# Key bias, mask stores, zeros' products and the router norm's small rows moved in a one-core perceiver kernel

## The chip, the cores and the metric

One Trainium2 chip, one NeuronCore of it. The metric is the device time of one execution in microseconds (us). The kernel of before ran three times: 1151.5 is the median, 1147.58 the lowest, 1159.3 the highest. A profile of one further execution gives every instruction's start and duration. The engines are PE (TensorE; its weight loads are listed as PEld), DVE (VectorE), ACT (ScalarE), POOL (GpSimd) and SP (SyncE, which here issues DMAs).

## The reference, cut to what matters

All in F32. 64 sequences of 32 tokens of 256 features attend to a context of 257 rows of 64 features; two layers of cross attention, self-attention and feed-forward, each ahead of a residual sum and behind a layer norm:

```python
x = x + _L0_xattn_ref(_layernorm(x), ctx_512, ...)
x = x + _L0_attn_ref(_layernorm(x), ...)
x = x + _L0_ffn_ref(_layernorm(x), ...)
x = x + _L1_xattn_ref(_layernorm(x), ctx_512, ...)
x = x + _L1_attn_ref(_layernorm(x), ...)
x = x + _L1_ffn_ref(_layernorm(x), ...)
```

Three of them matter here. `_L0_ffn_ref` picks 4 of 16 blocks of hidden units for each token and masks the others:

```python
prob = jax.nn.softmax(xf @ Wr.T + br, axis=-1)
_, idx = jax.lax.top_k(prob, TOP_K)
mask = mask.at[jnp.arange(n)[:, None], idx].set(1.0)
h = jax.nn.gelu(h, approximate=False) * mask[:, :, None]
```

`_L1_attn_ref` adds a bias to its queries, keys and values (`kg = einsum(x, Wk) + bk`). `_L1_ffn_ref` sends each token to one of 8 experts:

```python
route = jax.nn.sigmoid(x @ router_w)
max_ind = jnp.argmax(route, axis=1)
...
    h = jax.nn.silu(x @ gate_w[e]) * (x @ up_w[e])
    out = out + jnp.where(mask, h @ down_w[e], 0.0)
out = out * max_prob
```

## The kernel before, in words

The 2048 tokens are 16 tiles of 128 (NT = 16), taken in 4 groups of 4 tiles. The stages follow each other on one core, with the times of the profiled execution: first cross attention (to about 129 us), first self-attention with the feed-forward of group 0 woven in (to about 483), the feed-forward of groups 1 to 3 (to about 560), second cross attention in 32 pairs of batches (to about 905), second self-attention with the router (to about 1030), the experts (overlapping it from about 1018), and the last output DMAs.

The order of instructions on PE, DVE and ACT is the order of the source in these stages (`manual_schedule`). POOL's order is also that of the source in the two attentions of the first layer; in the second cross attention and the router POOL's order is not written by hand, and a scheduler chooses it. SP's DMAs wait in one queue.

What the change touches:

*Zeros' products.* `fill(n, bank)` (L562) issues n products of a 128x256 tile of zeros into a PSUM bank that nobody reads. It is called at the start of the first cross attention and in its first steps. Its main loop (L603) runs over t = 0 to 17. A step issues the scores of tile t + 1, a part of the next group's queries and keys, the output projection of tile t − 2 (`ya`, L552), the softmax's row sums, the transposes of tile t − 1's probabilities (`ptp_a`, L280, copied by ACT to `pT_a`, L282), the values of tile t + 1, and the product of probabilities and values of tile t − 1 (`oa`, L523, copied by ACT to `oTa`, L531). In the last steps tiles run out, so less work stands between these. Keys of the next stage are transposed there too (`kTp`, L392).

*Mask stores.* `choose_store(g)` (L705) transposes group g's mask of chosen blocks on PE (`mTp`, L710), copies it on DVE (`mTc`, L712) and stores it to DRAM (`maskd`, L713); `spread` loads it back as 8 broadcast tiles `mb`. A table filled by `at(slot, place, fn)` puts such steps into the slots t = 0 to 16 of the first self-attention's loop (L1136): group 0's store is in slot 9, group 1's in slot 13, both at place 2, which is between the ACT exponential and the output projection `yb` (L979) of tile t − 1. `oTb` (L971, DVE; L973, ACT) is that projection's input. Group 2's store is inside the last tile's projection, after head 11 of 16. The mask itself is finished by `choose_best` (L703 is its last addition).

*Key bias.* `e_bk` (L1725) multiplies the key bias, loaded as small DMAs into `e_b`, with a two-column mask, once, on POOL. The source puts it at pair 20 of the second cross attention. The keys' feature step of the next stage reads it (ACT, `kde`, L1452). In that same cross attention POOL negates each batch's row maximum (`nm`, L1516), which ACT's exponential (`pp`, L1519) uses as a bias; PE then transposes the probabilities (`pt`, L1547), and makes the next pair's queries (`qd`, L1306) and values' products (`np`, L1282).

*Router norm.* The router's layer norm works by groups of four (tiles 0 to 3) or two tiles. `route_stats(t)` makes statistics on DVE; with the last tile of a group it calls `route_scale` (L1793): POOL adds epsilon (L158), takes the power −1/2 (L159), copies the scale into `lnq_f` (L1799), makes minus mean times scale (L1800, L1801) and copies both per tile into the two extra columns of `xf`'s row (L1803), which is sent later to the sorted rows in DRAM. `route_norm` (called a step or more later, at a place of its own in the source) then makes `xn_f` on ACT (L1812) from `lnq_f`; `route_turn` transposes it on PE (`tpf`, L1828) and copies it on ACT (`xTf`, L1833); `route` makes the logits (`lpf`, L1842) and the one-hot choice on DVE (L1851 to L1862); `places` makes each token's rank in its expert on PE (`rank`, L1876), and `send` scatters the row by a POOL DMA (L1896). `give_table` makes on DVE the table of which expert each tile of sorted rows belongs to; its loads follow. `rows_turn` transposes the sorted rows (`tps`, L2214).

Of the kernel before, what the change touches and what calls it, by code (L numbers as in the profile page):

```python
# [7 lines left out]
F32 = mybir.dt.float32  # L8
# [31 lines left out]
def bc(ap, axis, n):  # L40

    shape = list(ap.shape)
    shape.insert(axis, n)
    return ap.unsqueeze(axis).to_broadcast(shape)
# [3 lines left out]
def perceiver_kernel(ctx: ExitStack, tc: tile.TileContext, a: dict, out: bass.AP):  # L48
# [22 lines left out]
    def sm(name, shape):  # L71
        return small.tile(shape, F32, tag=name.split("_")[0], name=name)
# [327 lines left out]
    with tc.tile_pool(name="wA", bufs=2) as work, tc.tile_pool(  # L400
# [75 lines left out]
        def power(t):  # L476
            nc.scalar.activation(sc[t], sc[t], AF.Exp)
# [84 lines left out]
        def fill(n_, bank=warm):  # L562
            for _ in range(n_):
                nc.tensor.matmul(bank, zero[:, 0:P], zero, start=True, stop=True)
# [38 lines left out]
        for t in range(NT + 2):  # L603


            if t + 1 < NT:
                score(t + 1)
            if t == 0:
                for part in (2, 3):
                    norm(1, part, "a", mvs, lat)  # L610
            if t == 2:
                fill(3, ps1.tile([P, 256], F32, tag="PT", name="warm2"))
            group(t // 4 + 1, (2, 0, 1, 3)[t % 4])
            for step in first.get(t, ()):
                step()
            if t > 1:
                project(t - 2)
            if t < NT:
                share(t)
            if t < 2:  # L620
                fill(2 - t)
            if 1 <= t <= NT:
                turned[t - 1] = heads_on_partitions(sc.pop(t - 1), ps1, t - 1, work, "a")
            if t + 1 < NT:
                values(t + 1)
                power(t + 1)
            if 1 <= t <= NT:
                gather(t - 1)
            if t == 14:
                keys_scale(0)  # L630
            if t == 15:
                turn_keys(0, ps2)
            norm(t // 4 + 2, t % 4, "a", mvs, lat)
            if 4 <= t < 11:
                norm_b(t - 4)
            if t == 10:
                rotate_last(work)
# [218 lines left out]
    with tc.tile_pool(name="wB", bufs=2) as work, tc.tile_pool(  # L856
# [118 lines left out]
        def project(t):  # L975
            oT = ctxo.pop(t)
            y_ps = outs[t] = ps_y.tile([P, D], F32, tag="y", name=f"yb{t}")
            for h in range(NH):
                nc.tensor.matmul(  # L979
                    y_ps, oT[:, h, :], b_o[:, h, :], start=(h == 0), stop=(h == NH - 1)  # L980
                )
                if (t, h) == (NT - 1, 11):
                    choose_store(NG - 2, ps2, work)

        def norm_stats(t):
# [68 lines left out]
        def at(slot, place, fn):  # L1054
            steps.setdefault((slot, place), []).append(fn)
# [10 lines left out]
        for g in range(NG - 1):  # L1066
            at(4 * g + 5, 5, lambda g=g: choose_norm(g))
            at(4 * g + 6, 1, lambda g=g: choose_turn(g, ps2, work))
            at(4 * g + 7, 5, lambda g=g: choose_blocks(g, ps2, work))
            if g == NG - 2:  # L1070
                at(4 * g + 8, 5, lambda g=g: choose_best(g, work, (2, 3)))
                continue
            for slot, place_, rounds in ((7, 5, (0,)), (8, 5, (1, 2)), (8, 4, (3,))):
                at(
                    4 * g + slot,
                    place_,
                    lambda g=g, rounds=rounds: choose_best(g, work, rounds),
                )
            at(4 * g + 9, 2, lambda g=g: choose_store(g, ps2, work))
        ff, late = {}, []  # L1080

        def ff_late():
# [312 lines left out]
    with wd1:  # L1395
        wd.close()
        with tc.tile_pool(name="wD", bufs=2) as work, tc.tile_pool(
# [290 lines left out]
            for pair in range(NB // 2):  # L1688


                b = 2 * pair
                if pair % 2 == 0 and pair // 2 + 2 < NT:
                    rotated(pair // 2 + 2)
                if pair == 0:
                    query_part(-1)
                    chain_n(1, ps1)()
                if pair == 3:
                    wdn.close()
                    mbw.close()
                    wc.close()  # L1700
                    wep = ctx.enter_context(tc.tile_pool(name="wep", bufs=1, side="right"))
                    fgp = ctx.enter_context(tc.tile_pool(name="fgp", bufs=1, side="right"))
                    fw.append(fgp.tile([P, NE * FE], F32, name="fg"))
                    we0 = ctx.enter_context(ExitStack())
                    e_w = we0.enter_context(tc.tile_pool(name="wE0", bufs=2, side="right"))
                    vd = [
                        e_w.tile([P, 4, 4, 4, NH + 1], F32, name=f"vde{z}", bufs=1)
                        for z in range(3)
                    ]
                if 2 < pair < 31:  # L1710
                    project((pair - 3) // 2, 4 * ((pair - 3) % 2), 4)
                if pair == 31:
                    project(NT - 2)
                for fn in behind.get(pair - 1, ()):
                    fn()
                turn(b)
                query_part(pair)
                for fn in front.get(pair, ()):
                    fn()
                turn(b + 1)  # L1720
                between(pair + 1)
                if 11 < pair < 28:
                    load_piece()
                if b == 40:
                    nc.gpsimd.tensor_tensor(e_bk, bc(e_b[:, 1], 2, 2), bc(mask2, 1, KC), ALU.mult)  # L1725
                if b == 16:

                    e_q = wep.tile([P, KC, D], F32, name="e_q")
                    by_pairs(e_q, a["e_wq"])
                    e_k = wep.tile([P, KC, D], F32, name="e_k")  # L1730
                    for k in range(KC):
                        for z in range(4):
                            o, w = divmod(z, 2)
                            nc.sync.dma_start(
                                e_k[:, k, o * P : (o + 1) * P].rearrange(
                                    "p (r w d) -> p w r d", r=4, w=2
                                )[:, w],
                                a["e_wk"][k * P : (k + 1) * P, :].rearrange(
                                    "p (r d) -> p r d", r=4
                                ),  # L1740
                            )

                    e_b = wep.tile([P, 2, KC], F32, name="e_b")
                    for z, v0 in enumerate((V_BQ, V_BK)):
                        for o in range(KC):
                            for r in range(4):
                                p0 = 64 * (r % 2) + 32 * o
                                nc.sync.dma_start(
                                    e_b[32 * r : 32 * r + 32, z, o : o + 1],
                                    a["vecs"][p0 : p0 + 32, v0 + r // 2 : v0 + r // 2 + 1],  # L1750
                                )
                    e_bk = wep.tile([P, KC, 2], F32, name="e_bk")
                    e_v = wep.tile([P, KC, DC], F32, name="e_v")
                    nc.sync.dma_start(e_v, a["e_wv"].rearrange("(k p) o -> p k o", p=P))
                    f_r = wep.tile([P, KC, 8], F32, name="f_r")
                    nc.sync.dma_start(f_r, a["f_wr"].rearrange("(k p) o -> p k o", p=P))
# [36 lines left out]
    def route_scale(ts):  # L1793

        n_ = len(ts)
        mv = rows[ts][:, 0:n_, :]
        sc2 = rows[ts] = sm(f"lnq_f{ts[0]}", [P, 4, 2])
        rs = rstd_of(mv, n_, f"f{ts[0]}", True)
        nc.gpsimd.tensor_copy(sc2[:, :n_, 0], rs)  # L1799
        nc.gpsimd.tensor_tensor(rs, rs, mv[:, :, 0], ALU.mult)  # L1800
        nc.gpsimd.tensor_scalar(sc2[:, :n_, 1], rs, -1.0, None, ALU.mult)  # L1801
        for i, t in enumerate(ts):
            nc.gpsimd.tensor_copy(xf[t][:, D + 2 : DP], sc2[:, i, :])  # L1803

    def route_norm(ts, pool=None):
        sc2, rows[ts] = rows[ts], []
        for i, t in enumerate(ts):
            if pool is None:
                y = xnp.tile([P, D], F32, tag="xn", name=f"xn_f{t}")
            else:  # L1810
                y = pool.tile([P, DP], F32, tag="r", name=f"xn_f{t}", bufs=7)[:, :D]
            nc.scalar.activation(  # L1812
                y, xs[t], AF.Identity, scale=sc2[:, i, 0:1], bias=sc2[:, i, 1:2]
            )
            rows[ts].append(y)
# [802 lines left out]
```

## Time and profile before

| | us |
|---|---|
| median of three runs | 1151.5 |
| lowest, highest | 1147.58, 1159.3 |
| the profiled execution | 1156.52 |
| its span, first to last instruction | 1154.6 |
| PE busy | 1106.7 |
| DVE busy | 767.8 |
| ACT busy | 572.7 |
| POOL busy | 463.9 |

The mean granted TensorE clock of the profiled execution is 0.986 of full speed. In the page, a row of the timeline is start, duration, engine, line, operation, output<-inputs, shape, number of instructions, and in brackets the idle time of the engine before it and what ended it. A row of the windows is the stretch, its length, the busy time of PE, PEld, DVE, ACT and POOL with instruction counts, the granted clock, the DMA share and GB/s. A row of the waits is engine and line that waited, what it waited for, the total, how often, and the longest. Matmuls of several instructions are shown as one row with their number behind an x.

The row maximum's negation L1516 on POOL and the exponential on ACT are among the costliest groups (128 and 256 instructions). 7 of L1799, L1800 and L1801 and 16 of L1803 run, between 949.6 and 1033.0.

### The profile page before, as it was taken

The numbers are of one execution on the slowest core, as the hardware profiler recorded it, in microseconds if no ns is written. First come the engines' busy times: TensorE is split into PE (matmuls) and PEld (weight loads), VectorE is DVE, ScalarE is ACT, GpSimd is POOL, SyncE is SP. The second block draws the span as 40 slices with busy tenths as digits, with TensorE's granted clock in tenths as the row PEclk, the third lists the DMA queues.
The fourth block names the chain that finished last, engine by engine and source line by source line (L and its number), as shares of the span: only waits on it lengthen the run. The fifth ranks groups of instructions, "written<-read, shape, count | busy, mean of one in ns | idle before, by whom it ended". The sixth has DMA issues, their size and how long they took to land. (4 is left out here: it accounts for less than half of the span.)

```text
span 1154.6 us, 26411 instructions
## 1 busy us (share of the span) xinstructions
PE 1106.7 (96%) x10036; PEld 792.2 (69%) x10036; DVE 767.8 (67%) x1805; ACT 572.7 (50%) x1433; POOL 463.9 (40%) x778
## 2 busy tenths in 40 slices
PE   9999999999999999999998999999999989889997
PEld 5667867777767657677776777777776656555653
DVE  5787156776987997655236787777878565765532
ACT  2346363545355365232236777777777556542221
POOL 1444266878768687410011121121222355642111
PEclk9999899999999999999999999999999988999999
DMA  5131142545436436591232121223220044212413
GB/s 134 58 95 40 33 124 82 176 126 168 120 109 200 129 106 191 159 257 36 74 83 22 29 55 29 74 56 83 64 76 19 17 125 122 85 36 73 154 39 117
DMA packets 98990, 109.05 MB, mean 94 GB/s; under 512 B 37240, under 2 KB 73465, under 8 KB 98642
## 3 DMA queue, kind: packets, MB, share of 16 engines
q1 hardware_dynamic: 97138, 103.05, 31.5%
q0 software_dynamic: 1728, 4.33, 1.1%
q8 instruction: 80, 1.31, 0.5%
q14 instruction: 44, 0.36, 0.1%
HBM read 76.36 MB, written 31.41 MB: 93 GB/s over the span
## 5 line engine op out<-in xcount | busy, mean ns | idle before, releaser
L1519 ACT ACTIVATE pp<-Sd,nm 128x256 f32<-128x256 f32 x256 | 119.9, 482 | 42.4 <-POOL nm L1516 42.4
L888 PEld LDWEIGHTS qb<-xT_b,b_q 128*128 128x128 f32 x512 | 94.7, 190 | 39.0 <-issue 18.5
L888 PE MATMUL qb<-xT_b,b_q 128*128 128x256 f32 x512 | 121.3, 385 | 0.0
L1516 POOL TENSOR_SCALAR nm<-nm 128x2 f32<-128x2 f32 x128 | 27.0, 211 | 219.4 <-DVE nm L1515 219.2
L979 PE MATMUL yb<-b_o,oTb 128*128 128x256 f32 x512 | 113.6, 380 | 0.5 <-DVE oTb L971 0.5
L1515 DVE TENSOR_REDUCE nm<-Sd 128x2 f32<-128x512 f32 x128 | 79.5, 683 | 50.1 <-PE Sd L1502 50.1
L979 PEld LDWEIGHTS yb<-b_o,oTb 128*128 128x128 f32 x512 | 96.2, 190 | 14.4 <-issue 1.4
L1537 DVE TENSOR_TENSOR pp<-pp,rd 128x512 f32<-128x512 f32 x128 | 89.6, 700 | 4.4
L1553 ACT COPY pTd<-pt 128x512 f32<-128x512 f32 x128 | 68.8, 591 | 10.0 <-PE pt L1547 4.2
L896 ACT COPY qTb<-qb 128x512 f32<-128x512 f32 x64 | 37.5, 585 | 69.8 <-PE qb L888 67.0
L1547 PE MATMUL pt<-cst,pp 128*128 128x128 f32 x512 | 67.8, 273 | 4.4 <-DVE pp L1537 1.7
L907 POOL TENSOR_TENSOR q2b<-qTb 128x512 f32<-128x512 f32 x64 | 64.7, 1042 | 14.6 <-ACT qTb L896 14.6
L1547 PEld LDWEIGHTS pt<-cst,pp 128*128 128x128 f32 x512 | 59.1, 141 | 13.8 <-ACT ld L1527 4.0
L941 DVE RECIPROCAL rqb<-rqb 128x512 f32<-128x512 f32 x16 | 53.5, 3344 | 17.8 <-ACT rqb L936 17.8
L1306 PE MATMUL qd<-xT_d,d_m 128*128 128x256 f32 x256 | 64.3, 395 | 0.7 <-DVE rd L1536 0.3
L1594 PE MATMUL yd<-d_n,co 128*128 128x256 f32 x256 | 63.2, 391 | 0.0
L1528 POOL TENSOR_TENSOR sd<-sd,ld 128x2 f32<-128x2 f32 x128 | 26.9, 210 | 86.0 <-ACT ld L1527 86.0
L1502 PE MATMUL Sd<-ct,qTd 64*128 64x256 f32 x480 | 60.0, 388 | 0.0
L1568 PE MATMUL od<-pTd,na 128*64 128x256 f32 x480 | 58.4, 385 | 0.0
L742 PE MATMUL yc<-c,hc 128*128 128x256 f32 x256 | 58.4, 381 | 0.0
L1594 PEld LDWEIGHTS yd<-d_n,co 128*128 128x128 f32 x256 | 46.2, 189 | 16.7 <-DVE nm L1515 7.7
L955 DVE RECIPROCAL rdb<-denb 128x512 f32<-128x512 f32 x16 | 53.7, 3355 | 5.8 <-PE denb L953 5.6
(433 smaller groups left out, 2426.9 us busy)
## 6 DMA issues: line engine op xcount, KB each, us to landing
srt<-pad SPq DMA_DIRECT2D x17, 1040.0 KB
mb<-maskd SPq DMA_DIRECT2D x64, 128.0 KB
ct<-ctd SPq DMA_DIRECT2D x30, 257.0 KB
rct<-in_ctxT_dram SPq DMA_DIRECT2D x32, 128.5 KB
rrt<-in_ctxT_dram SPq DMA_DIRECT2D x64, 64.2 KB
ctd<-rct SPq DMA_DIRECT2D x32, 128.5 KB
nad<-rna SPq DMA_DIRECT2D x16, 256.0 KB
fg<-in_f_wg_dram SPq DMA_DIRECT2D x16, 256.0 KB
```

The lines of the kernel that those rows point to most:

```text
L742: nc.tensor.matmul(y_ps, hs[f][:, i * P : (i + 1) * P], c_2[:, f, :], start=(f == 0), stop=(f == 7),)
L888: nc.tensor.matmul(q_ps[:, hh, :], b_q[:, k, h * P : (h + 1) * P], xT[:, k, c0 : c0 + 256], start=(k == 0), stop=(k == KC - 1),)
L907: nc.gpsimd.tensor_tensor(q2[:, 4 * h4 : 4 * h4 + 4, :], q, q, ALU.mult)
L979: nc.tensor.matmul(y_ps, oT[:, h, :], b_o[:, h, :], start=(h == 0), stop=(h == NH - 1))
L1306: nc.tensor.matmul(q_ps[:, r, :], m[:, k, pr * P : (pr + 1) * P], xT[:, k, c0 : c0 + 256], start=(k == 0), stop=(k == KC - 1),)
L1502: nc.tensor.matmul(logits[b][hh][:, u, :], qT[hs, b % 8, 4 * u : 4 * u + 4, :], ct[hs, b % 4, :KEYS], start=True, stop=True,)
L1515: nc.vector.tensor_reduce(nm, s_ps[hh], AX.X, ALU.max, negate=True)
L1519: nc.scalar.activation(pb[:, u, hh, :], s_ps[hh][:, u, :], AF.Exp, bias=nm[:, u : u + 1], accum_out=sd[:, u : u + 1],)
L1537: nc.vector.tensor_tensor(pp, pp, bc(rd, 2, KEYS), ALU.mult)
L1547: nc.tensor.transpose(pts[c][:, hh * 256 + u * P : hh * 256 + u * P + P], probs[b][:, u, hh, c * P : (c + 1) * P], ident,)
L1553: nc.scalar.copy(pT[:, c, :], pt)
L1594: nc.tensor.matmul(y_ps, co[:, pr, :], n[:, pr, :], start=(pr == pr0), stop=(pr == pr0 + n_pr - 1),)
```

## The change: what it does

Four parts. First, at step 14 of the first cross attention's loop a spare PSUM tile is allocated, and pairs of zeros' products go ahead of `project(13)` and, at steps 14 and 15, ahead of the product of probabilities and values: six products of 128x256. Second, the mask stores of groups 0 and 1 go one slot later, and that of group 2 after head 15 in place of head 11. Third, the key bias's product goes from POOL to DVE. Fourth, `route_scale` keeps only the addition and the power on POOL; the copy of the scale, the shift (now one instruction in place of two) and the row copies go to DVE, and stand at the head of `route_norm`.

The diff:

```diff
@@ first cross attention, loop over t
+            if t == 14:
+                spare = ps1.tile([P, 256], F32, tag="S", name="warm3")
+            if t == 15:
+                fill(2, spare)
             if t > 1:
                 project(t - 2)
...
+            if t in (14, 15):
+                fill(2, spare)
             if 1 <= t <= NT:
                 gather(t - 1)
@@ first self-attention, project(t)
-                if (t, h) == (NT - 1, 11):
+                if (t, h) == (NT - 1, NH - 1):
                     choose_store(NG - 2, ps2, work)
...
-            at(4 * g + 9, 2, lambda g=g: choose_store(g, ps2, work))
+            at(4 * g + 10, 2, lambda g=g: choose_store(g, ps2, work))
@@ second cross attention
                 if b == 40:
-                    nc.gpsimd.tensor_tensor(e_bk, bc(e_b[:, 1], 2, 2), bc(mask2, 1, KC), ALU.mult)
+                    nc.vector.tensor_tensor(e_bk, bc(e_b[:, 1], 2, 2), bc(mask2, 1, KC), ALU.mult)
@@ route_scale and route_norm
-        sc2 = rows[ts] = sm(f"lnq_f{ts[0]}", [P, 4, 2])
-        rs = rstd_of(mv, n_, f"f{ts[0]}", True)
-        nc.gpsimd.tensor_copy(sc2[:, :n_, 0], rs)
-        nc.gpsimd.tensor_tensor(rs, rs, mv[:, :, 0], ALU.mult)
-        nc.gpsimd.tensor_scalar(sc2[:, :n_, 1], rs, -1.0, None, ALU.mult)
+        rows[ts] = mv, rstd_of(mv, n_, f"f{ts[0]}", True)
+
+    def route_norm(ts, pool=None):
+        n_ = len(ts)
+        mv, rs = rows[ts]
+        sc2, rows[ts] = sm(f"lnq_f{ts[0]}", [P, 4, 2]), []
+        nc.vector.tensor_copy(sc2[:, :n_, 0], rs)
+        nc.vector.scalar_tensor_tensor(
+            sc2[:, :n_, 1], mv[:, :, 0], -1.0, rs, ALU.mult, ALU.mult
+        )
         for i, t in enumerate(ts):
-            nc.gpsimd.tensor_copy(xf[t][:, D + 2 : DP], sc2[:, i, :])
-
-    def route_norm(ts, pool=None):
-        sc2, rows[ts] = rows[ts], []
+            nc.vector.tensor_copy(xf[t][:, D + 2 : DP], sc2[:, i, :])
         for i, t in enumerate(ts):
```

Behind the new lines, line numbers in the changed program are higher: by 4 and 6 from the first cross attention's loop on, by 8 from the router's norm on.

## The prediction

> **What bounds the kernel now.** I read the page's first two parts, then the view of waits for PE, then the windows in which PE is not full, and the timeline at each wait that the change touches.
>
> ```profile
> PE 1106.7 (96%) x10036; PEld 792.2 (69%) x10036; DVE 767.8 (67%) x1805; ACT 572.7 (50%) x1433; POOL 463.9 (40%) x778
> ...
> PEclk9999899999999999999999999999999988999999
> ```
> ```profile
> PE mTp L710 <- DVE maskc L703: 3.9, 2, 2.1
> PE tpf L1828 <- ACT xn_f L1812: 2.5, 2, 2.3
> PE pt L1547 <- ACT ld L1527: 1.6, 1, 1.6
> PE oa L523 <- ACT pT_a L282: 1.3, 2, 0.7
> PE ya L552 <- ACT oTa L531: 1.1, 1, 1.1
> ```
>
> PE is busy 1106.7 of a span of 1154.6, so 47.9 us of idle is all that shorter waits can give. The second row says that busy is not all work: in some slices the granted clock is below full, and the same matmul lasts longer. The waits (total, times, longest) are short and scattered; those shown are the ones at the edited lines, 10.4 us together. So each edit is worth its own wait plus what the clock loses near it. One execution took 1156.52 around that span, 5.0 above the median of 1151.5; the sum below is made on 1156.5 and then moved to the median.
>
> **Zeros' products at the end of the first cross attention.**
>
> ```profile
> 117.99 1.70 PE L552 MATMUL ya<-a_o,oTa 128*128 128x256 f32 x4 [1.08 <-ACT oTa L531]
> 119.48 1.06 PE L280 MATMUL ptp_a<-cst,s_a 128*128 128x128 f32 x4
> 121.22 1.92 PE L523 MATMUL oa<-pT_a,vda 128*64 128x32 f32 x32 [0.68 <-ACT pT_a L282]
> 123.07 1.12 PE L392 MATMUL kTp<-cst,kvb 128*128 128x128 f32 x4
> 123.98 1.65 PE L552 MATMUL ya<-a_o,oTa 128*128 128x256 f32 x4
> 125.47 0.60 PE L280 MATMUL ptp_a<-cst,s_a 128*128 128x128 f32 x4
> ```
> ```profile
> 120.00:130.00 10.00, 9.32 (x93) 7.87 (x92) 2.16 (x6) 1.92 (x4) 1.05 (x1) 0.74 0.00 0
> ```
>
> The times ahead of PE are start and duration. The window's row gives, after the five busy times, the granted clock: 0.74. The ptp group takes 1.06 at 119.48 and 0.60 at 125.47; at full clock ya takes 1.03, oa 1.12 and kTp 0.60. Three pairs of zeros go into the waits for pT_a and oTa. A 128x256 product takes 0.38, a pair 0.76; the waits filled are 0.65, 1.08 and 0.68, so a pair alone overshoots by 0.1 at two of them. If the pairs keep the clock full, 117.99 to 125.47 (7.48) becomes 1.03 + 0.60 + 0.76 + 1.12 + 0.60 + 1.03 = 5.14, a gain of 2.3. What follows is PE-bound query work, so it is carried. Bounds: the whole clock loss of the two windows from 110, (1 − 0.92)·10 + (1 − 0.74)·10 = 3.4; the other way, no effect on the clock and only the overshoot, +0.2. I take −2.3, because the same row shows the clock lost with gaps of no more than 1.08 us and the zeros remove just these.
>
> [...]
>
> **Key bias on VectorE.**
>
> ```profile
> 623.40 0.20 POOL L1725 TENSOR_TENSOR e_bk<-e_b,mask 128x4 f32<-128x4 f32 x1 [2.49 <-DMA f_r<-in_f_wr_dram]
> 623.57 0.21 POOL L1516 TENSOR_SCALAR nm<-nm 128x2 f32<-128x2 f32 x1
> 623.81 0.47 ACT L1519 ACTIVATE pp<-Sd,nm 128x256 f32<-128x256 f32 x1 [1.75 <-POOL nm L1516]
> 625.00 0.63 PE L1547 MATMUL pt<-cst,pp 128*128 128x128 f32 x4 [1.58 <-ACT ld L1527]
> 627.13 3.58 PE L1306 MATMUL qd<-xT_d,d_m 128*128 128x256 f32 x8 [0.16 <-DVE rd L1536]
> ```
>
> Nobody fixes POOL's order in this stage; the bias product (0.20) stood early in its queue and waited 2.49 for a load, with the row-maximum negation nm behind it. ACT waits 1.75 for nm, PE 1.58 for ACT and 0.71 for the next pair, then qd runs at a reduced clock, 3.58 against 1.97 elsewhere. From np to Sd the pair before takes 6.48 (612.20 to 618.68), this one 9.56 (622.39 to 631.95): 3.1 us to win. On DVE the product stands where the source has it, at pair 20, long after its loads have landed, and costs some 0.2 (POOL's row) on an engine that is 67% busy; nothing on PE waits for it there. I take −3.1; the other end is 0, if the next small load in the queue or another dip takes its place.
>
> **Mask stores one place later.** The four mask transposes take 0.60 of PE, the DVE copy behind them 0.67, and then SP's store and the mask loads follow one slot later.
>
> ```profile
> 408.56 0.60 PE L710 MATMUL mTp<-cst,maskc 128*16 128x128 f32 x4 [1.81 <-DVE maskc L703]
> 409.89 0.68 DVE L971 COPY oTb<-avb 128x512 f32<-128x512 f32 x1
> 410.71 2.56 PE L979 MATMUL yb<-b_o,oTb 128*128 128x256 f32 x11
> 481.57 0.60 PE L710 MATMUL mTp<-cst,maskc 128*16 128x128 f32 x4 [2.11 <-DVE maskc L703]
> ```
>
> Group 0: no PE wait before, the 0.60 only moves. SP's mask loads are needed slots later. Group 1: the wait of 1.81 goes, but the projection yb behind it needs oTb, whose DVE copies end at 410.57, and yb started at 410.71; what is late next is oTb, and the gain is nothing. One slot later the 0.60 falls into full PE work, against about 0.7 that the earlier DVE copies give back at the next transposes. Net 0, from −1.8 (the wait truly goes) to +0.8 (0.60 plus a 0.2 wait for the bank). Group 2: 2.11 is filled by the last four heads, which end 1.7 earlier; but ACT's order behind it becomes hidden 0, root, hidden 1, with two more activation-table loads of 1.28 each, so the third hidden product waits until about 489.4 and the hidden stage ends near 498.2 as now. Net 0, from −1.7 to +0.6. SP's store of the mask now stands behind the load of d_wo, needed only in the next stage but one.
>
> **Norm scale and shift on VectorE.** For seven groups of tiles POOL loses lnq's copy, product, negation and two or four row copies (0.18, 0.19, 0.24, 0.19 each): 37 rows, some 7.3 us of POOL. DVE gains 30 rows of about 0.15 to 0.17 (its 128x16 rows: 0.175; its casts: 0.146), 4.9 us. Add and power stay on POOL. What decides is place: POOL ran them as soon as the statistics were there; DVE runs them where route_norm stands in its fixed order, and ACT's xn_f waits for the first two.
>
> ```profile
> 954.74 2.08 ACT L1812 ACTIVATE xn_f<-x,lnq_f 128x256 f32<-128x256 f32 x4
> 1009.04 1.09 ACT L1812 ACTIVATE xn_f<-x,lnq_f 128x256 f32<-128x256 f32 x2 [5.01 <-POOL lnq_f L1801]
> 1009.69 0.33 PE L1828 MATMUL tpf<-cst,xn_f 128*128 128x128 f32 x1 [2.34 <-ACT xn_f L1812]
> 1032.86 1.09 ACT L1812 ACTIVATE xn_f<-x,lnq_f 128x256 f32<-128x256 f32 x2 [0.39 <-POOL lnq_f L1801]
> 1035.96 0.29 PE L1876 MATMUL rank<-oh,tri 128*128 128x16 f32 x2
> ```
>
> Replayed group by group. Tiles 0 to 3: DVE's place is behind mx_e, which ends 955.63, so xn_f starts 956.0 for 954.74; ACT's kde, the transposes and lpf behind it (PE already waits 0.26 and 0.53 there) go 1.3 later. Tiles 4, 5: DVE is done when ACT asks, 0. Tiles 6, 7: 984.73 becomes 985.75, kde follows, and rank, which already waits 0.91 for kde, is 1.0 later. Tiles 8, 9: DVE ends 991.97 instead of 991.74, 0.2. Tiles 10, 11: the wait of 5.01 on ACT and 2.34 on PE looks like the prize, but DVE reaches these rows only behind the table's chain, which ends 1009.17; two rows later it is 1009.55, and the index chain that PE's tps waits 1.81 for has six more rows: +0.75. Tiles 12, 13: xn_f behind the attention output, 1028.08 for 1025.98, ACT's xTs behind it and gs 0.6 later. Tiles 14, 15: DVE's place is behind the hidden product that ends 1033.98, xn_f 2.1 later, the router's exponential and one-hot with it, rank at 1037.85; 1.3 more than the shifts before. Sum 1.3 + 1.0 + 0.2 + 0.75 + 0.6 + 1.3 = +5.2. POOL's power is ready each time before DVE's place (1006.91, 990.85, 1031.99), so DVE does not stall. Bounds: if POOL were the only limiter, the 2.5 of tpf waits go (−2.5); above, two dips of the clock like that at 626, (3.58 − 1.97) + some 0.7 = 2.3 each, +10. I take the replay.
>
> **Sum.** −2.3 − 3.1 + 0 + 5.2 = −0.2 on 1156.5; on the median of 1151.5 that is **1151.3**.
>
> **Rivals.**
> *The router was limited by POOL* (chance 0.25): DVE's rows find gaps, xn_f comes earlier and the tpf waits vanish. For it: ACT's 5.01 behind POOL. Against it: DVE's own queue at 1009. Sum −2.3 − 3.1 − 2.5 = −7.9: 1143.6; if both mask waits also go, −11.4: 1140.1.
> *Slower: ACT is held by DVE's queue in the router, and PE's clock dips there* (0.20). The late xn_f makes gaps like that at 1009 in several steps, each with a dip: +10, so −5.4 + 10 = +4.6: 1156. It decides once the router's delay exceeds the 5.4 that the zeros and the bias give; beyond 16.9 it would be over 1% slower. For it: PE already waits for xn_f, kde and xTf. Against it: most of the delayed transposes have other PE work beside them.
> *The zeros do nothing for the clock* (0.10): +2.3 to +2.5 on the sum, 1153.7.
> *The forecast* (0.45): small gains in the first stage and at the bias, taken back in the router; its own range is 1148 to 1155.
>
> **How the numbers follow.** The ends of all bounds add to −3.4 − 3.1 − 3.5 − 2.5 = −12.5 and 0.2 + 0 + 1.4 + 10 = +11.6; not all fall one way, so 1142 to 1161 leaves out about 2 in 10, the median's own scatter of 1147.6 to 1159.3 counted in. 1% (about what a measurement of this kernel can tell from no change) is 11.5. Faster by more needs the first rival with both mask waits: 0.12. Slower by more needs the second at more than its price: 0.11. Within: 0.77.
>
> **What would show it.** Right: clock near 1.0 from 118 to 126 and ptp at 0.60; the bias gone from POOL and no 1.75 wait of ACT near 623; no wait at mTp but the same starts of yb and of the third hidden product; xn_f waiting for DVE's lnq rows, at 1009 and 1033 above all. Wrong: tpf starting earlier than in the rows above, relative to the router's start; a new load-bound wait on POOL in the second cross attention; or a clock that dips at other places than before, which the replay cannot see.

## The result, and the profile after

The changed kernel takes 1156.91 us (median; 1153.21 to 1160.95) beside 1151.61 of before (1144.84 to 1159.3): ratio 1.0041, 95% interval 1.0026 to 1.0056, so +4.7 us (3.0 to 6.4; here and below a ratio is turned into us on 1151.6). The forecast was −0.2. It is slower, by less than 1%.

Its profiled execution took 1156.99 with a span of 1155.2, against 1156.52 and 1154.6 before. The two spans are 0.6 apart, and the medians 5.3. Most of what follows is about that gap.

The page after, engines and granted clock:

```profile
PE 1106.5 (96%) x10048; PEld 789.4 (68%) x10048; DVE 778.0 (67%) x1836; ACT 574.9 (50%) x1435; POOL 461.2 (40%) x740
...
PEclk9999999999999999999999999999999999989999
```

In the second row a 9 means 0.9 of full speed or more, and all slices but one have it: the half clock of before around 118 is gone (granted clock 1.00 from 118 to 126, before 0.57), and so is the one at 627 (1.00 from 626 to 630, before 0.62); in the router it is still there (0.50 from 1006.05 to 1009.46). PE's waits after:

```profile
PE yb L985 <- DVE oTb L977: 2.8, 2, 2.3
...
PE tpf L1836 <- ACT xn_f L1820: 2.3, 2, 2.1
...
PE hp L733 <- ACT hc L740: 2.0, 3, 1.4
...
PE rank L1884 <- DVE oh L1868: 1.3, 2, 0.9
```

The waits at mTp (3.9, now 0.4) and at the first pt (1.6) are gone; in their place yb waits for oTb and hp for hc, as forecast, rank waits for the one-hot choice, and tpf still waits for xn_f, 2.1 at its longest.

The edited places, in order of time. Zeros' products, timeline of PE and the window:

```profile
117.61 1.03 PE L564 MATMUL warm<-zero 128*128 128x256 f32 x4
118.57 1.12 PE L523 MATMUL oa<-pT_a,vda 128*64 128x32 f32 x32
119.63 0.66 PE L392 MATMUL kTp<-cst,kvb 128*128 128x128 f32 x4
```
```profile
120.00:130.00 10.00, 10.00 (x77) 8.55 (x76) 1.53 (x3) 2.83 (x6) 1.93 (x9) 1.00 0.18 50
```

PE is full and the clock 1.00, where it was 0.74. The pair of zeros is four instructions here, and the next product starts 0.96 behind its start; the prediction had 0.76 for a pair. The key bias and the next queries:

```profile
621.08 0.63 PE L1553 MATMUL pt<-cst,pp 128*128 128x128 f32 x4 [0.38 <-DVE pp L1543]
621.87 1.97 PE L1312 MATMUL qd<-xT_d,d_m 128*128 128x256 f32 x8 [0.16 <-DVE rd L1542]
```

No wait for ACT, and qd takes 1.97 for 3.58. The mask stores:

```profile
406.70 1.53 PE L985 MATMUL yb<-b_o,oTb 128*128 128x256 f32 x6 [2.26 <-DVE oTb L977]
```

The wait of 1.81 at mTp became one of 2.26 at yb. The router, ACT and PE:

```profile
949.70 2.08 ACT L1820 ACTIVATE xn_f<-x,lnq_f 128x256 f32<-128x256 f32 x4 [1.10 <-DVE lnq_f L1810]
...
1003.59 0.93 DVE L1955 CAST tei<-tef 128x3 int32<-128x3 f32 x1
...
1005.53 0.16 DVE L1809 COPY lnq_f<-lnr_f 128x2 f32<-128x2 f32 x1
...
1005.79 1.09 ACT L1820 ACTIVATE xn_f<-x,lnq_f 128x256 f32<-128x256 f32 x2 [6.52 <-DVE lnq_f L1810]
...
1006.44 1.40 PE L1836 MATMUL tpf<-cst,xn_f 128*128 128x128 f32 x4 [2.10 <-ACT xn_f L1820]
```
```profile
1033.65 1.09 ACT L1820 ACTIVATE xn_f<-x,lnq_f 128x256 f32<-128x256 f32 x2 [1.75 <-DVE lnq_f L1810]
```
```profile
1036.49 0.37 PE L1884 MATMUL rank<-oh,tri 128*128 128x16 f32 x2 [0.93 <-DVE oh L1868]
```
```profile
1006.00:1009.40 3.40, 2.94 (x10) 2.07 (x10) 2.44 (x12) 2.64 (x6) 0.73 (x1) 0.51 0.17 42
```

ACT now waits for DVE's lnq rows: 1.10, 6.52 and 1.75 in these three groups. Behind the 2.10 that PE stands idle at 1004 the clock is half for 3.4 us (0.51 in the window), and the four transposes take 1.40; in the profile before they take 1.05 (1009.69 to 1010.74).

### The profile page after: what moved, and what is told of

The parts are those of the page before. It is cut to its first block, busy times and chain, and to the rows that moved or that the text cites. A ratio compares the mean times of both kernels' runs of the same rounds, so it can differ in the third digit from the quotient of the medians.

```text
span 1155.2 us, 26423 instructions
## 1 busy us (share of the span) xinstructions
PE 1106.5 (96%) x10048; PEld 789.4 (68%) x10048; DVE 778.0 (67%) x1836; ACT 574.9 (50%) x1435; POOL 461.2 (40%) x740
## 5 line engine op out<-in xcount | busy, mean ns | idle before, releaser
L1534 POOL TENSOR_TENSOR sd<-sd,ld 128x2 f32<-128x2 f32 x128 | 29.5, 231 | 86.1 <-ACT ld L1533 85.2
```

## The experiments

Two theories. Theory 1: the profiled execution of before was slower than most, and the clock dips that the zeros and the bias remove are not in every execution; the router's loss is near the replay. Theory 2: the dips are in every execution, the two gains are whole, and the router loses far more. A rival to both: the parts disturb one another.

**The four parts, each alone.** The edits are the four parts of the diff above, each on the kernel before:

```diff
+ fill(2, spare)   # three places                                  p_fills
- nc.gpsimd.tensor_tensor(e_bk, ...
+ nc.vector.tensor_tensor(e_bk, ...                                p_bias
- at(4 * g + 9, 2, ...        - (t, h) == (NT - 1, 11)
+ at(4 * g + 10, 2, ...       + (t, h) == (NT - 1, NH - 1)         p_masks
- nc.gpsimd.tensor_copy(sc2[:, :n_, 0], rs)   # and what follows
+ nc.vector.tensor_copy(sc2[:, :n_, 0], rs)   # in route_norm      p_route
```

> The kernel before with the zeros' products alone. Theory 1 (the profiled execution of before had clock dips that most of its executions lack): the median gains about 0.5 to 1, while this run's own profile has a full clock at 118 to 126. Theory 2 (the dip at 118 is in every execution of before, and the router loses more than the replay said): -2.3 us as in the prediction's first term. A ratio of 0.998 or below speaks for the second, 0.999 to 1.000 for the first.

Measured: 0.9997 (0.9976 to 1.0017), −0.3 us (−2.8 to +2.0).

> The kernel before with the key bias's product alone on VectorE. Theory 1: the wait of 1.75 us on ACT is there in every execution, but the half clock behind it is not; about -1.5. Theory 2: the whole 3.1 us, ratio 0.9973.

Measured: 0.9984 (0.9965 to 1.0003), −1.8 us (−4.0 to +0.3).

> The kernel before with the later mask stores alone. Theory 1 and the replay: 0, waits at mTp gone and yb and the third hidden product as late as before. Theory 2: up to +1, the loss that the two profiles show between 352 and 432 us.

Measured: 0.9998 (0.9977 to 1.0018), −0.2 us (−2.6 to +2.1).

> The kernel before with the router norm's scale, shift and row copies alone on VectorE. Theory 1: +5 to +7, as the replay (+5.2) and the two profiles between 950 and 1040 us (+6.7) have it. Theory 2: +9 to +10, what is left of the measured +4.7 when zeros and bias give their 5.4. Rival to both: below +3, and the loss is an interaction of the parts.

Measured, in 6 executions where the other edits have 12: 1.0079 (1.0059 to 1.0098), +9.1 us (6.8 to 11.3). The router alone loses more than the replay's 5.2. The gains come out smaller than their terms, but at −0.3 and −1.8 the intervals are too wide to exclude −2.3 or −3.1: the traces have to tell.

**The kernel before, profiled again**, with no edit.

> The kernel before unchanged, one more profiled execution. Theory 1 (the first profile of before fell on a slow execution, and its dips of the clock differ from one execution to the next): other dips than at 118, 627, 938 and 961, at least one of the edited places at full clock, span 1143 to 1150. Theory 2 (the dips belong to the kernel): the same dips, span 1153 to 1156.

> The kernel before unchanged, a second one of these. As for the first; the two are also told apart by whether 118 to 125 and 627 to 630 are at half clock in both.

Measured: 1154.13 and 1156.37. The spans, 1152.2 and 1154.5, are not as short as theory 1 asked. In both, the half clock at 36 and at 118 is gone (1.00 from 118 to 126) and there is one at 478 instead; the others, near 625, 938, 960 and 1016, lie within some 5 us of those of the first profile (0.66 and 0.71 from 626 to 630, where that has 0.62). So at the zeros' place theory 1 holds, at the bias's place theory 2. The first of the two, the same place as the rows in the prediction:

```profile
117.38 1.13 PE L552 MATMUL ya<-a_o,oTa 128*128 128x256 f32 x4 [1.08 <-ACT oTa L531]
118.34 0.60 PE L280 MATMUL ptp_a<-cst,s_a 128*128 128x128 f32 x4
119.62 1.13 PE L523 MATMUL oa<-pT_a,vda 128*64 128x32 f32 x32 [0.67 <-ACT pT_a L282]
```
```profile
120.00:130.00 10.00, 10.00 (x99) 8.64 (x96) 1.53 (x3) 2.50 (x5) 2.87 (x10) 1.00 0.12 30
```

The same waits of 1.08 and 0.67, and the clock is 1.00. Here zeros can only cost: from the ptp_a at 112.89 to the oa that follows the one above, at 123.58, is 10.69, and 10.86 in all six profiles with the zeros. In the first profile of before the same stretch (113.51 to 126.87) is 13.36. Over all profiles of kernels without the zeros, the clock between 118 and 126 is below 1.00 in 4 of 10 (0.57, 0.79, 0.79, 0.57), and the stretch takes 13.36, 12.04, 12.02 and 13.36 in these, 10.68 or 10.69 in the six others. So the zeros gain 2.5, 1.2 or −0.2, on the mean of these ten 0.6.

That the zeros are what keeps the clock full is not shown. None of the six profiles with them has half clock there, but the four that have it are exactly those that also have it at 36, ahead of everything that the change touches, and no profile with the zeros has it at 36. What speaks for the zeros is where the waits fall. In the first profile of before the half-clock stretches begin 24, 173, 264, 271 and 288 times 3.413 us behind the one at 36.5; in that of the changed kernel 7, 21 and 24 times behind the one at 934.4. In steps of this length, counted back from the half clock, the waits of 0.65 and 1.08 of the first profile lie in one step, 115.0 to 118.4, and half clock follows; in the second profile, counted back 149 steps from its half clock at 625.3 (0.83 from 620 to 630, 0.66 from 626), a step ends at 116.69 and cuts the 1.08 in two. The first row is of the first profile, the two others are of the second:

```profile
115.00:118.41 3.41, 1.68 (x42) 1.41 (x35) 2.39 (x10) 2.91 (x5) 1.05 (x1) 1.00 0.02 5
```
```profile
113.28:116.69 3.41, 2.37 (x66) 1.50 (x64) 3.18 (x11) 3.37 (x5) 1.05 (x1) 1.00 0.02 5
116.69:120.11 3.42, 2.06 (x25) 1.67 (x26) 1.55 (x5) 1.22 (x3) 0.12 (x1) 1.00 0.00 0
```

PE is busy for 1.68 of 3.41, or 0.49, ahead of the half clock, and for 0.69 and 0.60 where the clock stays full. In the four profiles with the dip the emptiest of these steps has 0.49 to 0.51, in five of the six without it 0.55 to 0.61 and in one 0.50; with the zeros PE is busy all the time (8.00 of 8.00 from 118 to 126 in all six). That the clock follows from this share is the author's reading, and no run tests it.

At the bias, between 626 and 630, the clock is below 1.00 in 7 of 9 profiles without the bias's move (0.62 to 0.74), in none of 7 with it. From the prediction's np to its Sd, 9.56 there, takes 6.46 or 6.47 in all seven with the move; without it 9.35 to 9.56 in six, 8.70 and 8.71 in two, and 6.84 in one: on the mean 2.5 more. The 6.84 is the mask stores alone, where POOL waited at the bias for 1.00 and not 2.49, and PE not at all for ACT:

```profile
621.40 0.20 POOL L1725 TENSOR_TENSOR e_bk<-e_b,mask 128x4 f32<-128x4 f32 x1 [1.00 <-DVE nm L1515]
```

The 8.71 is the run with all groups but tiles 10 and 11 (below), where the wait is there and the half clock is not, so that the wait alone costs 2.2:

```profile
621.23 0.63 PE L1547 MATMUL pt<-cst,pp 128*128 128x128 f32 x4 [1.97 <-ACT ld L1527]
...
623.35 1.97 PE L1306 MATMUL qd<-xT_d,d_m 128*128 128x256 f32 x8 [0.16 <-DVE rd L1536]
```

**Without the router's part, and only parts of it.**

```diff
  the changed kernel; route_scale and route_norm as before          p_noroute
+ LATE = (ROUTED[-3],)                     # tiles 10, 11 on DVE     p_route10
+ LATE = ROUTED[:-3] + ROUTED[-2:]         # all the others on DVE   p_rest
  p_route, with:                                                    p_swap
+        route_norm(p10)
         give_table()
         loads_to(FIRST[1])
-        route_norm(p10)
```

> The changed kernel without its fourth part: zeros, key bias and mask stores as changed, the router norm's rows on GpSimd as before. Theory 1 (the dips that the zeros and the bias remove are there in some executions only): the sum of the three parts measured alone, about -2.3 us, ratio 0.998. Theory 2: -5.4 us, ratio 0.9953. Rival: the parts disturb one another and it is no faster than before.

Measured: 0.9993 (0.9972 to 1.0014), −0.8 us (−3.2 to +1.6). Theory 2's −5.4 is outside; theory 1's −2.3 is inside.

> The kernel before with the rows of tiles 10 and 11 alone on VectorE. Theory 1 (this group carries the undershoot of the replay): +3 to +4 us where the replay said +0.75, with xn_f 2 us later against the scores' start, an idle PE of about 2.2 us ahead of tpf and a half clock behind it. Theory 2 (the loss is spread over all groups, or comes from the number of rows on VectorE): +0.5 to +1.5.

Measured: 1.0016 (0.9993 to 1.0039), +1.8 us (−0.8 to +4.5): no verdict by the time.

> The kernel before with the rows of all groups but tiles 10 and 11 on VectorE. Theory 1: +4.5 us, the replay's sum without that group (5.2 - 0.75), perhaps 1 more for the gap ahead of the logits of tiles 4 and 5. Theory 2: +7 to +8.

Measured: 1.0041 (1.0019 to 1.0063), +4.7 us (2.2 to 7.3), as theory 1 had it.

> The kernel with the router norm's rows alone on VectorE, where for tiles 10 and 11 they stand ahead of the table's chain in VectorE's order and not behind it; nothing else differs from the run of that part alone (+9.1). Theory 1 (place in the queue is the cost): xn_f some 2 us earlier, no idle PE over 1 us ahead of tpf, +5 to +6. Rival (the engine is the cost: VectorE's rows disturb the others wherever they stand): still +9.

Measured: 1.0051 (1.0027 to 1.0074), +5.9 us (3.1 to 8.5), as theory 1 had it, but its interval meets that of +9.1.

The traces tell the groups apart better than the times, for they show each shift at its place. Starts of the same PE product, less those of the run without the router's part, both counted from the same product at 945:

| what moves | groups on DVE | on POOL | the prediction |
|---|---|---|---|
| lpf of tiles 0 to 3 | +1.07 | 0.01 | +1.3 |
| tiles 4, 5: from there through their lpf and scores | +0.9 | 0.2 | 0 |
| rank of tiles 4, 5 to tpf of tiles 6, 7 | +0.85 | 0 | +1.0 |
| tiles 6, 7: lpf; tiles 8, 9: rank | −0.47, +0.44 | 0 | +0.2 |
| tiles 10, 11: scores to tps | +2.0, +2.4, +3.3 | 0 | +0.75 |
| the same, rows ahead of the table | +0.2, +0.4 | | |
| tiles 12, 13: gs | +0.3 | 0 | +0.6 |
| tiles 14, 15: rank | +1.16 | 0 | +1.3 |

The columns are read from eight profiles. Five have most groups on DVE: the changed kernel, p_route, p_rest, p_swap and p_after_swap. In four of them the shifts outside tiles 10 and 11 agree to 0.1; in p_swap a dip at 987 lies over some. One has tiles 10 and 11 alone (+2.4), and two have POOL (p_before_a, p_fillbias). "Rows ahead of the table" are p_swap and p_after_swap; in p_rest, which has these two tiles on POOL, the shift is 0. Together the shifts are 6.3 to 7.6. Behind the router, at 1045, the changed kernel is 7.3 later than the run without the part and p_route 8.0; the seven other profiles with the unshortened rows on POOL are 0 to 2.5 later, by their half clocks.

**Two more: the change with that one move, and the parts that measured below zero.**

```diff
  the changed kernel, with route_norm(p10) ahead of give_table()     p_after_swap
  before + zeros + bias                                              p_fillbias
  before + bias, and in route_scale                                  p_pool
- rs = rstd_of(mv, n_, ...);  nc.gpsimd.tensor_copy(sc2[:, :n_, 0], rs)
+ rs = sc2[:, :n_, 0]      # epsilon and power written there
  p_pool + zeros                                                     p_best
```

> The changed kernel, with the rows of tiles 10 and 11 ahead of the table's chain in VectorE's order. Theory (the place of these rows in VectorE's queue is the term that the replay undersized): 2 to 3.5 us less than the changed kernel's +4.7, so +1 to +3, ratio about 1.002, and PE waits for xn_f there by less than 1 us. Rival (the wait only moves to the index chain that the sorted rows' transposes need, which now stands behind four more rows): +4 to +5.

Measured: 1.0017 (0.9991 to 1.0043), +2.0 us (−1.0 to +5.0), beside +4.7 (3.0 to 6.4) of the change. Its ACT and PE rows:

```profile
1001.06 1.09 ACT L1820 ACTIVATE xn_f<-x,lnq_f 128x256 f32<-128x256 f32 x2 [4.26 <-DVE lnq_f L1810]
```
```profile
1001.80 0.95 PE L1836 MATMUL tpf<-cst,xn_f 128*128 128x128 f32 x4
```

From the scores' start (997.03) xn_f is 4.03 away, where the changed kernel has 1005.79 − 999.50 = 6.29; PE no longer waits for it. In p_swap it is 3.78 away, and PE does not wait there either. So for these tiles the place in DVE's order was the cost, and not the engine; the index chain behind took only +0.4.

> The kernel before with zeros' products and key bias alone. Theory 1: -2 to -3 us, the sum of the two alone (-0.3 and -1.8) and of the shares of executions in which their dips occur. Theory 2: -5.4. Rival: the 0.7 that the three parts together gave.

Measured: 0.9978 (0.9958 to 0.9998), −2.5 us (−4.8 to −0.2).

> The kernel before with the key bias on VectorE, and the router norm's rows on GpSimd as before but one instruction shorter (the power is written into the scale's column, so the copy goes). Theory 1 (xn_f is late by GpSimd's own queue at tiles 8 to 11 and nothing behind it is worth more than 0.3): -2 to -3, hardly more than the bias alone (-1.8). Rival (GpSimd is the router's limiter): -4 or more.

Measured: 0.9968 (0.9944 to 0.9993), −3.7 us (−6.4 to −0.8). With p_fillbias it is one of two versions whose interval lies wholly below the kernel before; both were measured beside a median of before of 1153.54, where the other sets of runs had 1151.24 to 1151.89. How much of it is the copy's, beyond the bias's −1.8, the intervals do not tell.

> The kernel before with the zeros' products, the key bias on VectorE and the router norm's rows on GpSimd without the scale's copy: the parts that measured below zero. Theory 1: -3 to -4, the bias's -1.8 to -2.6, some 1 of the zeros and up to 1 for the copy; ratio 0.997. Theory 2 (the terms in full): -5.5 or more. Rival (parts are not additive, as three of them together gave only -0.7): about -1.

Measured: 0.9979 (0.9955 to 1.0003), −2.4 us (−5.2 to +0.3): no better than p_pool, though the interval holds theory 1's −3 to −4 too.

## Why the prediction was wrong

**The first step that failed: the zeros' term (−2.3) as part of a sum for the median.** It was read correctly from the one execution: between the two profiles the stretch shrinks by 2.5. But it was half clock, and with the same waits no half clock came there in 6 of 10 profiles, where the zeros cost 0.2. On the mean of the profiles the term is −0.6, and alone it measured −0.3 (−2.8 to +2.0). The prediction knew that its profile lay 5.0 above the median, and moved the sum by that; it should have asked which of its own terms the 5.0 contained.

**The second: tiles 10 and 11, +0.75.** The traces show +2.0 to +3.3. The replay put the new rows behind the table's chain, which was right, but took the chain's end from the first profile: 1009.17, which is 4.49 behind the start of the scores and hardly later than POOL's rows. That profile is the exception. In it the 64 score products run through; in the 15 others PE stands still among them ("issue" in the rows: no releaser that the profile shows), DVE's softmax rows and the chain follow later, and the chain ends 5.87 to 6.71 behind the scores' start. The scores' start in the first profile, then the scores, the end of the chain and ACT's xn_f in the run of the mask stores, which has the rows on POOL:

```profile
1004.68 1.05 PE L311 MATMUL S_e<-kde,qTe 32*32 32x64 f32 x64
```
```profile
996.52 0.70 PE L311 MATMUL S_e<-kde,qTe 32*32 32x64 f32 x46
997.54 0.32 PE L311 MATMUL S_e<-kde,qTe 32*32 32x64 f32 x5 [0.31 <-issue]
998.29 0.39 PE L311 MATMUL S_e<-kde,qTe 32*32 32x64 f32 x13 [0.44 <-issue]
```
```profile
1002.43 0.17 DVE L1962 CAST rowi<-row 128x3 int32<-128x3 f32 x1
```
```profile
1000.83 1.09 ACT L1812 ACTIVATE xn_f<-x,lnq_f 128x256 f32<-128x256 f32 x2 [4.79 <-POOL lnq_f L1801]
```

POOL's rows do not wait for the chain: xn_f starts 4.31 behind the scores here and 4.31 to 4.73 in all eight profiles with the unshortened rows of these tiles on POOL and an uneven run of scores. Behind DVE's chain it starts 6.21 to 6.31 behind (three profiles). So PE's wait grows from about 0.3 to 2.10 to 2.17. The first profile hid this, for PE stood idle there for 2.34 in any case. And behind the 2.10 of the changed kernel PE ran at half clock for 3.41 us (0.50 from 1006.05 to 1009.46); behind the 2.17 of p_route the four tpf take 1.40, where four at 994.57 in the same profile, behind a wait of 0.51, take 0.63. The prediction's own rival, a dip there, was priced at 2.3 and placed in the slower case.

**Other steps.** The bias's term was right within what can be told: −3.1 forecast, 2.5 on the mean of the traces, −1.8 (−4.0 to +0.3) measured. The rest of the router was near: 1.07, 0.85, 0.3 and 1.16 for 1.3, 1.0, 0.6 and 1.3, and together +4.7 (2.2 to 7.3) for 4.45. Only tiles 4 and 5, +0.9 for 0, were missed, for another reason: 64 small products ve, in one piece without the router's part, stand still twice in it, with no releaser that the profile shows. The run with the rows ahead of the table, then the one without the router's part:

```profile
970.46 0.31 PE L2094 MATMUL ve<-e_v,xT_e 128*32 128x64 f32 x4 [0.20 <-issue]
971.17 0.44 PE L2094 MATMUL ve<-e_v,xT_e 128*32 128x64 f32 x12 [0.40 <-issue]
```
```profile
971.71 1.10 PE L2092 MATMUL ve<-e_v,xT_e 128*32 128x64 f32 x64
```

PE stands still at this place in all five kernels with these groups on DVE, but also in p_pool, which has none there (0.43), and in none of the others profiled. So it is not the engine of the rows alone. The zeros move such a stop too: in all six kernels with them PE stands still for 0.5 to 1.6 near 921 behind the 59th of 64 ve, and in none of the ten without. What stops the issue was not tried, and stays open.

The mask stores cannot be told from their forecast of 0 by time: −0.2 (−2.6 to +2.1). In the traces group 0's transposes give 0.58 in their old slot and cost 0.85 in the new, group 1's add 0.6, +0.9 by 440; at the start of the next stage 1.7 is won and given back to the table loads, as forecast. So this term is +0.9, inside its bound of +1.4. One thing may take it back: half clock at 478, behind the wait of 2.11 that group 2's move fills, costs 1.7 in 7 of the 12 profiles without the move, and comes in none of the four with it. Whether the move prevents it is not shown.

The rival "the router was limited by POOL" fell by the traces: xn_f came later on DVE, not earlier. Where the rows stand ahead of the chain (3.78 and 4.03 behind the scores) it comes some 0.5 earlier than from POOL, and PE's wait of 0.3 goes, but no more. The run with one instruction less on POOL, −3.7 (−6.4 to −0.8), does not decide it. "The zeros do nothing for the clock" stays open where there is a dip; in 6 of 10 profiles there was none to remove. The slower rival came true in its mechanism, ACT held by DVE's queue, at one place more than by several dips. That its price, +4.6, is nearly the measured +4.7 is luck: it had +10 for the router and −5.4 for the gains.

An estimate from the means and shifts above: −0.6 for the zeros, −2.5 for the bias, +0.9 for the mask stores and +6.3 to +7.6 for the router make +4.1 to +5.4 (1.0 less if the mask stores' move does prevent the half clock at 478), beside +4.7 (3.0 to 6.4) measured. The parts need not disturb one another for that: the same terms give −3.1 for zeros and bias and −2.2 with the mask stores, inside the intervals of −2.5 (−4.8 to −0.2) and −0.8 (−3.2 to +1.6). That they do not disturb one another is not shown either.

## What to carry to other kernels

Half clock in one profile was a chance here, not a term: profile the kernel several times before its dips enter a sum. The dip at the zeros came in 4 of 10 profiles, the one at the bias in 7 of 9. When small rows moved from POOL, which ran them as soon as it could, to DVE with its fixed order, what counted was their place in that order, and not their duration: four rows worth 0.6 us cost 2 to 3 behind a chain and 0.4 ahead of it. The end of that chain, too, has to be read from more than one profile: 4.49 behind the scores' start in the first, 5.87 to 6.71 in the others.

## What the runs showed of the hardware

In the first profile of before and in that of the changed kernel the granted clock is 1.00 or 0.50. At 0.50 it stays for 3.41 us (from 36.49, 626.99 and 1019.53 before; from 934.37, 958.26 and 1006.05 after) or 6.83 (from 118.41, 937.61 and 961.50 before; from 1016.29 after), and from 1152.65 and 1152.82 to the end of the span. The waits of PE ahead of the one at 118.41 are 0.65 and 1.08, and in the 3.41 us ahead of it PE is busy for 0.49; in the second profile 3.41 us near that place have 0.60, and the clock behind them is 1.00. What decides the clock no run here tests. The executions of before differ by 14 us (1144.8 to 1159.3), and with 0.998 at 1147.0 and 0.982 at 1159.0 their mean clock differs too.

In the changed kernel some DVE instructions of a few elements last longer where they fall beside POOL's 128x512 subtraction (1.04 to 1.06). The row copies have a median of 0.16; three that start within 0.02 of a subtraction (949.70, 979.60, 986.67) last 1.05, 1.06 and 1.07. tei, which starts 0.13 behind one there and 0.14 behind one in p_route, lasts 0.93 in both, and 0.17 in the run of the mask stores, where no subtraction runs beside it.
